# Two small setup products as 32-output matmuls, a label multiply placed earlier on GpSimd, and VectorE's first clears in pieces

## The chip, the cores and the metric

The kernel runs on one core of a Trainium2 chip. The metric is the device time of one execution in microseconds, median over several runs. A core has a matrix engine (TensorE, PE in the profile, with its weight loads shown apart as PEld), three engines for element-wise work (VectorE or DVE, ScalarE or ACT, GpSimd or POOL), and SyncE (SP), which here only issues DMAs. Each engine takes its instructions in order; between engines they wait on semaphores.

## The reference

A graph-attention layer over B = 16 batches of N = 512 nodes with F = 512 features, H = 16 heads of 32, two directions d, and only the first 20 nodes of each batch as keys and values. All in fp32.

```
row_zero  = v.sum(-1) == 0
q_exp     = where(row_zero, 0, q)                      # the condition, per node
self_feat = concat(v, q_exp) @ W_self.T + b_self
for d in 0, 1:
    A    = adj (or its transpose)[:, :, :20, :]        # 11 labels per pair
    cond = A.sum(-1);  vb = A @ w_bias + b_bias
    kv   = self_feat[:, :20]
    aff  = (self_feat @ Wq.T + bq) . (kv @ Wk.T + bk) / sqrt(32)   # per head
    aff  = where(cond > 0, aff, -9e15) + vb
    w    = softmax(aff over the 20 keys)
    out += per head: (w @ kv) @ Wout + bout
result = v + relu(self_feat + out)
```

The labels `adj` (the mask input) are integers; the sum over labels and the weighted sum with `w_bias` are needed for each batch.

## The kernel before, in words

The order of work on every engine is the order in which the code is written; no scheduler changes it. The first 90 us are the setup, after which a loop over the batches runs.

The setup has these steps:

- *Key rows* (L775 to L831). `xkv` holds the 320 key rows (16 x 20), transposed. GpSimd adds its four chunks into `rsk`. TensorE multiplies the rows with `W_self` (`kv_terms`, L781, weights 128 wide, 320 columns), the condition with its part of `W_self` (L791, four groups of 16 outputs into `ps_q`), then sums `rsk` over the partitions with a matrix of ones (L795, into `ps_nk`: every output row is the same sum). ScalarE copies `ps_q` into `q4` (L797). TensorE selects from `q4` with a 0/1 matrix `sel` (L800, one matmul for each of C = 4 chunks, 16 columns), which turns the condition round so that features lie on partitions. VectorE makes `nzk`, the flag of a nonzero key row (L798), copies the selection into `qw` (L801), and with products `qp` (L807) joins it to the key rows: `kvn` (L811), and `kvD`, differences to the first key (L815). TensorE goes on with the last five `kv_terms` and then with the key projections `key_rows` (L831, groups of four matmuls with 32 outputs each).
- *Bursts* n = 0 to 19 (the loop `for n, runs in enumerate(bursts)`). Each burst folds the projected keys into Wq (`keys`, L930, into a pair of PSUM tiles), ScalarE and VectorE copy the result to a stage `st` (L952, L954), and SyncE stores a finished stage to DRAM, `g_d` (L959, L961). There are sixteen stages (fc, hg); those with hg = 0, 1, 2 share three buffers in turn. Between the bursts stands other work, dealt out by the string `plan`: "v" and "w" make values (L893), "c" makes key biases (`bias_scores`: ScalarE's copy L871, GpSimd's sum L875, four small stores L877 to `cq_d`), "n" the row flags, "p" the self products of batch 0.
- *Batch 0's masks.* `mask_mul(0, 0)` turns the labels into floats on ScalarE (L323) and multiplies them by `w_bias` on GpSimd (L324); `mask_count` sums the labels on VectorE (L332) and GpSimd writes the -9e15 terms (L333); `mask_sum` reduces on VectorE (L338). `load_cq` (L128, SyncE) brings the key biases back from `cq_d`.
- *Blocks.* `clear_first` (L154) clears a DRAM area `bd_d` with one DMA issued by GpSimd; `spill` (L193, from n = 14 on, on GpSimd's and SyncE's queues) copies the values `vw_d` into it.

The first instructions on VectorE are three clears: `ones`, one half of `ps_q`, and `bqbd` (L723 to L726); `ones` starts seven warm-up matmuls on TensorE (L737).

Of the kernel before, what the change touches and what calls it, by code (L numbers as in the profile page):

```python
# [13 lines left out]
P = 128  # L14
# [4 lines left out]
def gat_kernel(  # L19
# [20 lines left out]
    nc = tc.nc  # L40
    B, F, N = xT.shape
    NG, L = adj.shape[3], adj.shape[4]
    H, DH = 16, 32
    C = F // P
    HL = P // DH
# [105 lines left out]
    def clear_first():  # L151

        n = C * EARLY * 32 // P
        nc.gpsimd.dma_start(  # L154
            bd_d[0].rearrange("c b r e i g -> (c b r) (e i g)").rearrange("(n p) w -> p n w", p=P),
            zero.unsqueeze(1).to_broadcast([P, n, HL * 2 * DH]),
        )
# [9 lines left out]
    def blocks(n):  # L167

        found = []
        bb = bd_d[n].rearrange("c b r e i g -> (c b) r e i g")  # L170
        vv = vw_d[n].rearrange("d c (b m) (e g) -> d (c b) m e g", m=NG, e=HL)
        for e in range(HL):
            for i in range(2):
                j = (e * S) // 32 + i
                for d in range(2):
                    lo = max(e * S + d * NG, 32 * j)
                    hi = min(e * S + (d + 1) * NG, 32 * j + 32)
                    if lo < hi:
                        m, r = lo - e * S - d * NG, lo - 32 * j
                        found.append((bb[:, r : r + hi - lo, e, i], vv[d, :, m : m + hi - lo, e]))  # L180
        return found
# [133 lines left out]
    def mask_mul(b, h, labels=range(11)):  # L315
        a = adjs[b, h].rearrange("p t (m l) -> p (t m) l", l=L)
        if labels[0] == 0:
            prods[b, h] = (msk if h == 0 or b == 0 else xsum).tile(
                [P, 2 * S, L + 1], F32, tag="prod", name=f"prod{b}_{h}", bufs=1
            )  # L320
        p = prods[b, h]
        if b == 0:
            nc.scalar.copy(p[:, :, :L], a)  # L323
            nc.gpsimd.tensor_mul(p[:, :, :L], p[:, :, :L], wb_sb.unsqueeze(1).to_broadcast([P, 2 * S, L]))  # L324
        else:
            for l in labels:
                nc.scalar.activation(p[:, :, l], a[:, :, l], AF.Identity, scale=wb_sb[:, l : l + 1])  # L327
# [371 lines left out]
    with tc.tile_pool(name="setup", bufs=1) as sp, tc.tile_pool(name="ps_acc", bufs=4, space=PSUM) as acc["pool"]:  # L699
# [18 lines left out]
        with tc.tile_pool(name="setup_k", bufs=1) as sk:  # L718
# [3 lines left out]

            nc.vector.memset(ones, 1.0)  # L723
            ps_q = ps_s.tile([P, 2, 512], F32, tag="s0", name="ps_q4", bufs=1)
            nc.vector.memset(ps_q[:, 0], 0.0)
            nc.vector.memset(bqbd, 0.0)  # L726
            nc.gpsimd.memset(zero, 0.0)

            nc.gpsimd.memset(sel, 0.0)
# [62 lines left out]
                    ps_q[bass.ds(k * DH, B), 0], q_sb[:, k], ws_q[:, k], start=True, stop=True  # L792
                )
            ps_n = ps_s.tile([P, 2, 512], F32, tag="s1", name="ps_nk", bufs=1)[:, 0]
            nc.tensor.matmul(ps_n[:, :BM], ones, rsk, start=True, stop=True)  # L795
            q4 = sk.tile([P, F], F32, name="q4")
            nc.scalar.copy(q4, ps_q[:, 0])  # L797
            nc.vector.tensor_scalar(nzk, ps_n[:, :BM], 0.0, None, ALU.not_equal)  # L798
            for c in range(C):
                nc.tensor.matmul(ps_q[:, 1, bass.ts(c, B)], q4[:, bass.ts(c, P)], sel, start=True, stop=True)  # L800
            nc.vector.tensor_copy(qw, ps_q[:, 1, : C * B].rearrange("p (c b) -> p c b", b=B))  # L801
            for fc, k in ((0, 3), (1, 3), (2, 3), (3, 2), (3, 3)):
                kv_terms(fc, k)
# [56 lines left out]
        with tc.tile_pool(name="setup_g", bufs=3) as sg:  # L860
# [60 lines left out]
            def keys(runs):  # L921


                pairs = [ps_s.tile([P, 2, 512], F32, tag=f"s{i}", name=f"ps_g{runs[0]}{i}", bufs=1) for i in range(2)]
                at = 0
                for fc, hg, d, lo, hi in runs:
                    n = (hi - lo) * ND
                    for hl in range(HL):
                        r = bass.ts(hl, DH)
                        nc.tensor.matmul(  # L930
                            pairs[hl // 2][:, hl % 2, at : at + n], wq_sb[r, d, hg, bass.ts(fc, P)],
                            khD[r, d * C + hg, lo * ND : hi * ND], start=at == 0, stop=True, skip_group_check=True,
                        )
                    at += n
                if not units and runs is bursts[-1]:
                    for hl in range(HL):
                        r = bass.ts(hl, DH)
                        nc.tensor.matmul(
                            pairs[hl // 2][:, hl % 2, at:], wq_sb[r, 0, 0, :P], khD[r, 0, : 512 - at],
                            start=False, stop=True, skip_group_check=True,  # L940
                        )
                at = 0
                for fc, hg, d, lo, hi in runs:
                    n = (hi - lo) * ND
                    if (fc, hg) not in stages:
                        stages[fc, hg] = (late if hg == C - 1 else sg).tile([P, B, HL, 2, ND], F32, tag="st", name=f"st{fc}{hg}")
                    st = stages[fc, hg]
                    for half in range(2):
                        to = st[:, lo:hi, bass.ts(half, 2), d].rearrange("p b h m -> p h b m")
                        of = pairs[half][:, :, at : at + n].rearrange("p h (b m) -> p h b m", m=ND)  # L950
                        if half == 0:
                            nc.scalar.activation(to, of, AF.Copy, scale=SCALE)  # L952
                        else:
                            nc.vector.tensor_scalar(to, of, SCALE, None, ALU.mult)  # L954
                    at += n
                    if d == 1 and hi == B:
                        to, of = g0[:, fc, bass.ts(hg, WD // C)], st[:, 0].rearrange("p h d m -> p (h d m)")
                        nc.gpsimd.tensor_copy(to, of)
                        nc.sync.dma_start(g1_d[C * fc + hg], st[:, 1].rearrange("p h d m -> p (h d m)"))  # L959
                        if fc * hg < (C - 1) * (C - 1):  # L960
                            nc.sync.dma_start(g_d[C * fc + hg], st[:, 2:])  # L961
# [44 lines left out]
            for n, runs in enumerate(bursts):  # L1006
                for i in range(len(rest)):
                    if (i < 1 and n > 0) or any(fc == 0 and (d, hg) == rest[0] for fc, hg, d, _, _ in runs):
                        key_rows(*rest.pop(0))
                if n in (3, 4):  # L1010
                    values(*steps["v"].pop(0)[1])
                if n == 0:
                    bo_rows = load.tile([P, C, N], F32, tag="x2", name="bo_rows", bufs=1)
                    nc.sync.dma_start(bo_rows[:, :2], bout.partition_broadcast(P))
                keys(runs)
                if n == 8:
                    mask_count(0, 0)
                if n == 14:
                    mask_count(0, 1)
                if n == 17:  # L1020
                    mask_sum(0, 1)
                value_pieces()
                if rest:
                    for kind in "mm" if n else ():
                        f, args = steps[kind].pop(0)
                        f(*args)
                    continue
                first = n if first is None else first
                for kind in plan[n - first] if n - first < len(plan) else ():
                    f, args = steps[kind].pop(0)  # L1030
                    f(*args)
                    if kind == "w":
                        value_pieces()
                if n == first:
                    for d in range(2):
                        nc.gpsimd.tensor_add(br_sb, br_sb, bo_rows[:, d])
                if n > first:
                    value_pieces()
                if n == 7:
                    mask_mul(0, 0)  # L1040
                if n == 10:
                    mask_sum(0, 0)
                    load_cq(0)
                if n == 7:
                    clear_first()
                if n == 9:
                    row_sums(1)
                    copies = blocks(0)
                if n > 13:
                    spill(1, nc.gpsimd)  # L1050
                    spill(1)
                if n == 11:
                    mask_mul(0, 1)
                    new_self(0)
                    for i in range(1, 5):
                        x_sum(0, i)
                if 10 < n < 15:
                    mask_spread(0, 0, (n - 11,))
                if n == 16:
                    gs[0] = g0  # L1060
                    key_sum(0, 1)
                    load_adj(1, 0)
                if n == 18:
                    mask_spread(0, 1)
                    key_bias(0)
                    load_adj(1, 1)
                    load_cq(1)
# [357 lines left out]
```

## Time and profile before

| | |
|---|---|
| time, median of 3 runs | 549.41 us (548.23 to 549.83) |
| the profiled execution | 548.23 us, its span 546.2 us |
| TensorE busy | 540.2 us, 99% of the span |
| VectorE, ScalarE, GpSimd busy | 481.3, 404.1, 434.3 us |
| granted TensorE clock | 0.996 of full |
| bytes moved by DMA | 126.45 MB, 232 GB/s over the span |

In the rows of a timeline stand the start in us, the busy time in us, the engine, the line, the operation and what it writes and reads, how many were merged, and in brackets how long the engine had been idle before and what ended that. Rows of groups give the busy time and the mean of one instruction in ns. SPq and POOLq are DMA queues by the engine that issues. In the rows of windows each engine has its busy time in the stretch and, in brackets, how many of its instructions touch it; the last three numbers are the granted clock, the share of the DMA engines' time, and GB/s.

### The profile page before, as it was taken

How to read it: one execution, taken by the hardware profiler on the slowest of the kernel's cores; microseconds unless marked ns; L12 is line 12 of the kernel's file. 1: busy time of each engine (PE TensorE's matmuls, PEld its weight loads, DVE VectorE, ACT ScalarE, POOL GpSimd, SP SyncE). 2: the span in 40 equal slices, each digit the busy share in tenths (PEclk: the TensorE clock that was granted, in tenths of full speed). 3: DMA queues.
4: the chain of work that ended last, by engine and by line, in shares of the span. 5: the costliest groups of instructions: out<-in, count | busy, mean ns of one | idle time of the engine just before them, and what ended most of it. 6: DMA issues, size and time to landing. Idle time of an engine off the chain costs nothing.

```text
span 546.2 us, 19673 instructions
## 1 busy us (share of the span) xinstructions
PE 540.2 (99%) x7932; PEld 423.7 (78%) x7932; DVE 481.3 (88%) x711; ACT 404.1 (74%) x999; POOL 434.3 (80%) x418
## 2 busy tenths in 40 slices
PE   9999999999999999999999999999999999999996
PEld 6544368889888878787888878887878788878784
DVE  1776678889999999999989999999999999999997
ACT  1225435888887979788888888888878787978664
POOL 2637996779979797979798888888897979797664
PEclk9999999999999999999999999999999999999998
DMA  8999999978886877878776758676777777736034
GB/s 306 377 396 355 314 360 342 311 259 251 226 255 190 250 194 225 227 217 233 220 219 192 236 180 232 203 231 188 231 210 210 194 230 191 240 92 200 2 116 156
DMA packets 100546, 126.45 MB, mean 232 GB/s; under 512 B 19608, under 2 KB 68694, under 8 KB 98408
## 3 DMA queue, kind: packets, MB, share of 16 engines
q1 hardware_dynamic: 98856, 122.19, 72.2%
q0 software_dynamic: 1168, 2.23, 1.8%
q8 instruction: 62, 1.02, 0.8%
q10 hardware_dynamic: 432, 0.79, 0.4%
q14 instruction: 28, 0.23, 0.1%
HBM read 86.23 MB, written 40.24 MB: 232 GB/s over the span
## 4 chain that ended last, share of the span: by engine, by line
PE 97%; DVE 2%; ACT 0%; issue 0%; DVEq 0%
PE ps_f L667 32%; PE ps_a L397 24%; PE ps_c L397 11%; PE ps_d L397 6%; PE ps_o_f L569 5%; PE ps_v L893 3%; PE ps_k L831 3%; PE ps_kv L781 2%; PE ps_a L284 1%; PE ps_o_c L569 1%; PE ps_l L397 1%; PE ps_c L284 1%; PE ps_warm L737 1%; PE ps_o_s L569 0%; DVE o L611 0%; DVE w L465 0%
## 5 line engine op out<-in xcount | busy, mean ns | idle before, releaser
L327 ACT ACTIVATE prod<-adj,wb_sb 128x80 f32<-128x80 int32 x330 | 116.0, 429 | 0.0
L537 POOL TENSOR_TENSOR w<-w,sm 128x640 f32<-128x640 f32 x63 | 80.3, 1275 | 33.0 <-DVE sm L533 29.3
L667 PE MATMUL ps_f<-t,ws_s 128*64 128x246 f32 x720 | 80.0, 370 | 0.0
L667 PEld LDWEIGHTS ps_f<-t,ws_s 128*64 128x64 f32 x720 | 51.7, 136 | 18.9
L528 ACT ACTIVATE w<-w 128x640 f32<-128x640 f32 x60 | 43.9, 731 | 18.0 <-DVE w L524 18.0
L545 DVE STREAM_TRANSPOSE wt<-w 128x640 f32<-128x640 f32 x63 | 52.5, 834 | 0.1
L667 PE MATMUL ps_f<-x,ws_v 128*64 128x246 f32 x480 | 52.4, 371 | 0.0
L532 DVE TENSOR_REDUCE sm<-w 128x32 f32<-128x640 f32 x63 | 51.1, 811 | 1.1 <-ACT w L528 0.8
L523 DVE TENSOR_REDUCE ps_d<-w 128x32 f32<-128x640 f32 x59 | 48.7, 826 | 1.8 <-ACT ps_d L431 0.2
L524 DVE TENSOR_TENSOR w<-w,ps_d 128x640 f32<-128x640 f32 x59 | 48.4, 821 | 2.0
L370 POOL TENSOR_TENSOR k<-g,k 128x608 f32<-128x608 f32 x30 | 44.8, 1492 | 0.0
L667 PEld LDWEIGHTS ps_f<-x,ws_v 128*64 128x64 f32 x480 | 34.7, 137 | 13.0
L397 PEld LDWEIGHTS ps_a<-g,sf 128*64 128x64 f32 x544 | 34.2, 137 | 5.9 <-issue 5.8
L397 PE MATMUL ps_a<-g,sf 128*64 128x152 f32 x544 | 38.6, 295 | 0.0
L397 PE MATMUL ps_d<-g,sf 128*64 128x152 f32 x544 | 37.9, 293 | 0.0
L346 ACT COPY both<-add 64x80 f32<-64x80 f32 x128 | 32.6, 254 | 5.7 <-DVE add L338 4.6
L569 PE MATMUL ps_o_c<-wt,vd 32*32 32x256 f32 (+1 forms) x720 | 36.8, 386 | 0.0
L338 DVE TENSOR_REDUCE add<-prod 128x80 f32<-128x960 f32 x32 | 36.7, 1146 | 0.0
L682 POOL TENSOR_TENSOR t<-x,t 128x492 f32<-128x492 f32 x30 | 34.9, 1163 | 1.2
L397 PEld LDWEIGHTS ps_d<-g,sf 128*64 128x64 f32 x544 | 35.3, 137 | 0.2 <-ACT sf L685 0.2
L333 POOL TENSOR_SCALAR prod<-cond 128x80 f32<-128x80 f32 x32 | 18.1, 566 | 21.7 <-DVE cond L332 20.2
L569 PE MATMUL ps_o_f<-wt,vd 32*32 32x256 f32 (+1 forms) x672 | 34.6, 386 | 0.0
(300 smaller groups left out, 1435.8 us busy)
## 6 DMA issues: line engine op xcount, KB each, us to landing
g<-g_d SPq DMA_DIRECT2D x60, 304.0 KB
g_d<-st SPq DMA_DIRECT2D x16, 1064.0 KB
out_T<-o SPq DMA_DIRECT2D x64, 256.0 KB
x<-in_xT SPq DMA_DIRECT2D x56, 256.0 KB
xn<-in_xn SPq DMA_DIRECT2D x48, 256.0 KB
adj<-in_adj SPq DMA_DIRECT2D x52, 220.0 KB
vd<-bd_d SPq DMA_DIRECT2D x64, 64.0 KB
nz<-nz_d SPq DMA_DIRECT2D x14, 256.0 KB
```

What stands on the lines that cost most here:

```text
L327: nc.scalar.activation(p[:, :, l], a[:, :, l], AF.Identity, scale=wb_sb[:, l : l + 1])
L338: done["masks"] = nc.vector.tensor_reduce(add, prods.pop((b, h)), AX.X, ALU.add)
L370: done["ksum"] = engine.tensor_sub(to, one, two)
L397: nc.tensor.matmul(slot(g)[bass.ts(p, P // 2), : HL * S].rearrange("p (h m) -> p h m", m=NG)[:, :, 1:], of(k)[:, bass.ds(first + g * P // ...
L523: nc.vector.tensor_reduce(mx, f, AX.X, ALU.max)
L524: done["weigh"] = (engine or nc.vector).tensor_sub(f, f, mx.unsqueeze(2).to_broadcast([P, per, NG]))
L528: done["exp"] = nc.scalar.activation(t, t, AF.Exp)
L532: nc.vector.tensor_reduce(sm, heads(weighs[b, c, l]), AX.X, ALU.add)
L537: done["normal"] = nc.gpsimd.tensor_mul(f, f, smalls.pop((b, c, l)).unsqueeze(2).to_broadcast([P, per, NG]))
L545: done["turn"] = nc.vector.transpose(wts[b][:, c, l], weighs.pop((b, c, l)).rearrange("p g w -> p (g w)"))
L569: nc.tensor.matmul(outsum[b][a][bass.ds(at // 2 * DH, n * DH), bass.ds(c * N // 2 + lo * R, (hi - lo) * R)].rearrange("p (n r) -> p n r", ...
L667: nc.tensor.matmul(parts[b][n in (2, 3, 5)][bass.ts(a, P // 2), bass.ts(i, HN)], lhs, x[:, k], start=False, stop=k == 1, skip_group_check= ...
```

## The change

Four edits in the setup:

- VectorE's clear of `ps_q` is made in four pieces of 128 columns, that of `bqbd` in four pieces.
- The sum of the key rows (L795) becomes four matmuls with 32 outputs each, and each of the four selecting matmuls (L800) becomes four with 32 outputs.
- `mask_mul(0, 0)` moves, within burst 7, from after the values' stores to right after `keys(runs)`.
- `clear_first()` moves from the end of burst 7 to burst 11.

```diff
             ps_q = ps_s.tile([P, 2, 512], F32, tag="s0", name="ps_q4", bufs=1)
-            nc.vector.memset(ps_q[:, 0], 0.0)
-            nc.vector.memset(bqbd, 0.0)
+            for a in range(HL):
+                nc.vector.memset(ps_q[:, 0, bass.ts(a, F // HL)], 0.0)
+            for c in range(C):
+                nc.vector.memset(bqbd[:, :, c], 0.0)
...
-            nc.tensor.matmul(ps_n[:, :BM], ones, rsk, start=True, stop=True)
+            for a in range(HL):
+                nc.tensor.matmul(ps_n[bass.ts(a, R), :BM], ones[:, :R], rsk, start=True, stop=True)
...
             for c in range(C):
-                nc.tensor.matmul(ps_q[:, 1, bass.ts(c, B)], q4[:, bass.ts(c, P)], sel, start=True, stop=True)
+                for a in range(HL):
+                    nc.tensor.matmul(
+                        ps_q[bass.ts(a, R), 1, bass.ts(c, B)], q4[:, bass.ds(c * P + a * R, R)], sel, start=True, stop=True
+                    )
...
                 keys(runs)
+                if n == 7:
+                    mask_mul(0, 0)
                 if n == 8:
                     mask_count(0, 0)
...
-                if n == 7:
-                    mask_mul(0, 0)
                 if n == 10:
                     mask_sum(0, 0)
                     load_cq(0)
-                if n == 7:
-                    clear_first()
                 if n == 9:
                     row_sums(1)
                     copies = blocks(0)
+                if n == 11:
+                    clear_first()
```

On TensorE, at the end of the key rows' products (ps_nk is the sum, the second ps_q row the selection; the sizes are outputs x columns). Before:

```order
L781 MATMUL ps_kv_185<-xkv,ws_v 128x320
L791 MATMUL ps_q_124<-ws_q,q_sb 16x512 x4
L795 MATMUL ps_nk<-rsk,ones 128x320
L800 MATMUL ps_q_124<-sel,q_204 128x16 x4
L781 MATMUL ps_kv_183<-xkv,ws_v 128x320
L781 MATMUL ps_kv_184<-xkv,ws_v 128x320
```

Now (the changed file's lines are 2 to 6 higher):

```order
L783 MATMUL ps_kv_191<-xkv,ws_v 128x320
L793 MATMUL ps_q_124<-ws_q,q_sb 16x512 x4
L798 MATMUL ps_nk<-rsk,ones 32x320 x4
L804 MATMUL ps_q_124<-sel,q_213 32x16 x16
L783 MATMUL ps_kv_189<-xkv,ws_v 128x320
L783 MATMUL ps_kv_190<-xkv,ws_v 128x320
```

The order is the same; the sum and the selection stand there as four and sixteen matmuls instead of one and four.

On GpSimd, in bursts 7 to 11 (the second key biases c and their stores to cq_d, the labels' product prod, the clear of bd_d, the row sums rx of batch 1). Before:

```order
L958 COPY g_84<-st_582 128x152
L875 TENSOR_TENSOR c<-c,bb_sb 128x320
L877 DMA cq_d<-c 4x16x20 x4
L324 TENSOR_TENSOR prod_0_648<-prod_0_648,wb_sb 128x80x11
L154 DMA bd_d_89<-zero 128x5x256
L958 COPY g_84<-st_625 128x152
L333 TENSOR_SCALAR prod_0_648<-cond_0_676 128x80
L913 DMA vw_d_88<-v_694 128x4x128
L215 TENSOR_TENSOR rx_728<-x_176 128x512
L217 TENSOR_TENSOR rx_728<-rx_728,x_176 128x512 x2
L913 DMA vw_d_88<-v_793 128x4x128
L324 TENSOR_TENSOR prod_1_796<-prod_1_796,wb_sb 128x80x11
```

Now:

```order
L964 COPY g_84<-st_603 128x152
L324 TENSOR_TENSOR prod_0_649<-prod_0_649,wb_sb 128x80x11
L881 TENSOR_TENSOR c<-c,bb_sb 128x320
L883 DMA cq_d<-c 4x16x20 x4
L964 COPY g_84<-st_646 128x152
L333 TENSOR_SCALAR prod_0_649<-cond_0_696 128x80
L919 DMA vw_d_88<-v_714 128x4x128
L215 TENSOR_TENSOR rx_748<-x_182 128x512
L217 TENSOR_TENSOR rx_748<-rx_748,x_182 128x512 x2
L919 DMA vw_d_88<-v_813 128x4x128
L154 DMA bd_d_89<-zero 128x5x256
L324 TENSOR_TENSOR prod_1_817<-prod_1_817,wb_sb 128x80x11
```

The product of the first labels moved ahead of the second key biases and their four stores, and the clear moved behind the row sums, to right before the second labels' product. On ScalarE the labels' cast (L323) likewise moved ahead of the copy of the second key biases (L871).

## The prediction

> **What bounds the kernel now.** I read the first part of the page, then the chain of waits, and only then the two stretches of the setup in which the edits lie.
>
> ```profile
> span 546.2 us, 19673 instructions
> PE 540.2 (99%) x7932; PEld 423.7 (78%) x7932; DVE 481.3 (88%) x711; ACT 404.1 (74%) x999; POOL 434.3 (80%) x418
> PE 97%; DVE 2%; ACT 0%; issue 0%; DVEq 0%
> ```
>
> TensorE is busy in 99% of the span and makes 97% of the chain that ended last. So an edit pays only by what it takes off TensorE's own sequence, or costs what it puts into it; time saved on VectorE, ScalarE or GpSimd is worth nothing unless TensorE waits for it. Next the chain and the timeline at 10 to 17 us, where the two matmul edits lie:
>
> ```profile
> 10.96 0.98 PE ps_q L791 x8
> 11.94 0.74 PE ps_nk L795 x2
> 12.68 1.03 PE ps_q L800 x8
> 13.71 2.79 PE ps_kv L781 x10
> ...
> 10.89 1.05 PE L791 MATMUL ps_q<-ws_q,q_sb 128*16 128x512 f32 x8
> 11.87 0.30 PEld L795 LDWEIGHTS ps_nk<-rsk,ones 128*128 128x128 f32 x2 [0.85 <-issue]
> 12.01 0.59 ACT L797 COPY q<-ps_q 128x512 f32<-128x512 f32 x1 [8.53 <-PE ps_q L791]
> 12.64 0.97 PEld L800 LDWEIGHTS ps_q<-sel,q 128*128 128x128 f32 x8 [0.48 <-ACT q L797]
> 12.72 0.49 DVE L798 TENSOR_SCALAR nzk<-ps_nk 128x320 f32<-128x320 f32 x1 [10.82 <-PE ps_nk L795]
> 13.53 2.46 PEld L781 LDWEIGHTS ps_kv<-xkv,ws_v 128*128 128x128 f32 x10
> 13.82 0.23 DVE L801 COPY qw<-ps_q 128x64 f32<-128x64 f32 x1 [0.62 <-PE ps_q L800]
> 15.21 0.97 DVE L815 TENSOR_TENSOR kvD<-kvn 128x304 f32<-128x304 f32 x1
> 16.43 1.18 PEld L831 LDWEIGHTS ps_k<-kvD,wk 128*32 128x32 f32 x24 [0.44 <-issue]
> ```
>
> Each fp32 matmul stands as two records. The selection (L800) can't begin before ScalarE's copy of q4 ends at 12.01 + 0.59 = 12.60; that is the one true wait here. After it come eight weight loads, and the key products' next load starts at 13.53.
>
> **The key rows' sum (L795).** One matmul with 128 outputs becomes four with 32 over the same 320 columns. Whatever it gains, 0.1 us or 0.3 us, TensorE then stands before the selection, which waits for q4 until 12.60, and q4 needs only L791. On TensorE's sequence it is worth 0. It would cost only from the point where the four end after 12.60, that is if they ran one after another: 3 more x 0.74 = 2.2 us. The groups of weight loads and two slices of 20 ns say that they do not:
>
> ```profile
> L831 PEld LDWEIGHTS ps_k<-kvD,wk 128*32 128x32 f32 x60 | 1.8, 110 | 2.1 <-issue 0.4
> L800 PEld LDWEIGHTS ps_q<-sel,q 128*128 128x128 f32 x8 | 1.0, 191 | 0.5 <-ACT q L797 0.5
> ...
> 16.46:16.48 0.02, 0.02 (x5) 0.02 (x8) 0.02 (x1) 0.00 (x0) 0.02 (x1) 1.00 0.28 102
> 16.50:16.52 0.02, 0.02 (x4) 0.02 (x8) 0.02 (x1) 0.00 (x0) 0.02 (x1) 1.00 1.42 512
> ```
>
> In the key products L831, which already have this 32-output form, eight loads and four matmuls are in flight 0.03 us after the first load began at 16.43: the four column groups run side by side.
>
> **The selection (L800).** Four matmuls of 16 columns become sixteen, each with a quarter of the weights: 32 records instead of 8. Before, eight loads take (13.53 - 12.64) / 8 = 0.111 us each; with only 16 columns to stream behind, the load is the cost. A 32-wide load lasts 110 ns against 191 ns, 81 ns less for 96 columns, so 0.84 ns a column: 27 ns of pure loading instead of 108, and about 4 ns beside it, 31 ns a record. From below: four groups side by side, 8 records each, 8 x 0.031 = 0.25 us. From above: no overlap at all, 32 x 0.031 = 1.0 us. In between lies the closest packing of small matmuls that the trace shows, in the chain:
>
> ```profile
> 35.70 0.10 PE _g(0, 2, 0, 14, 16)0_449 L930 x2
> 35.80 0.01 PE _g(0, 2, 0, 14, 16)1_450 L930 x2
> ```
>
> Four records of 38 columns in 0.11 us, 27 ns each, which would make 32 x 0.027 = 0.86 us. But those have 128-wide loads of 108 ns in four row groups, 108 / 4 = 27, so this is a load bound and not a pace of issue. I take 0.40 us, nearer to the lower end, since the loads at 16.43 start within 10 ns of each other.
>
> Behind it the array goes from 32-wide to 128-wide weights, which was not so before at this place. The price is in the rows above: the 128-wide load at 11.87 starts 0.07 us before the last 16-wide matmul ends (10.89 + 1.05 = 11.94), while the one at 13.53 starts 0.18 us before the selection's last ends (13.71). The switch costs 0.11 us. (The one before L795 goes away, but there q4 covers it.) So the next key products load at 12.64 + 0.40 + 0.11 = 13.15 instead of 13.53: **0.38 us off TensorE's sequence**; by the bounds 0.53 off or 0.22 on.
>
> Does the 0.38 last? What TensorE needs next is kvD at 16.43, now 16.05. VectorE's link starts with qw at 13.82, which follows the selection by 0.11 us and moves 0.38 to 0.49 earlier; nzk was done at 12.72 + 0.49 = 13.21 and is out of the way if the sum ends only 0.1 us sooner. kvD's first quarter, now ending at 15.21 + 0.97 = 16.18, comes at about 15.7. From there on the chain is TensorE's without a gap until the last 20 us, so the gain is carried to the end.
>
> **VectorE's clears.**
>
> ```profile
> 1.09 0.48 DVE L725 MEMSET ps_q<- 128x512 f32 x1
> 1.62 0.27 DVE L726 MEMSET bqbd<- 128x256 f32 x1
> ```
>
> Two become eight. If each piece cost as much as its whole, 4 x 0.75 = 3.0 us, VectorE would be done at 4.1 us; the first reader is L791 at 10.89 and VectorE's own next work is at 12.72. Cover of over 6 us: 0, gain or loss.
>
> **GpSimd's order at 55 to 76 us.** Here the multiply goes ahead of the second half of the key biases (sum L875 and four stores L877), and the clearing DMA goes behind the row sums.
>
> ```profile
> 55.04 0.72 POOL L875 TENSOR_TENSOR c<-c,bb_sb 128x320 f32<-128x320 f32 x1
> 56.06 2.55 POOL L877 DMA_DIRECT2D cq_d<-c  x4 [0.29 <-POOL c L875]
> 58.63 2.11 POOL L324 TENSOR_TENSOR prod<-prod,wb_sb 128x880 f32<-128x880 f32 x1
> 60.67 0.96 POOL L154 DMA_DIRECT2D bd_d<-zero  x1
> 68.81 2.11 POOL L324 TENSOR_TENSOR prod<-prod,wb_sb 128x880 f32<-128x880 f32 x1
> 72.00 1.14 POOL L257 TENSOR_TENSOR t<-x,t 128x492 f32<-128x492 f32 x1
> 85.94 0.31 POOL L958 COPY g<-st 128x152 f32<-128x152 f32 x1 [2.92 <-ACT st L952]
> ...
> 63.88 2.07 SPq L128 DMA_DIRECT2D cq<-cq_d  x2
> 66.07 1.65 SPq L959 DMA_DIRECT2D g_d<-st  x1
> 67.83 1.19 SPq L961 DMA_DIRECT2D g_d<-st  x1
> SPq L128 <- DMA cq_d<-c: 2.9, 1, 2.9
> bd_d<-zero POOLq DMA_DIRECT2D x1, 640.0 KB, 8.4
> 76.15 1.07 ACT L952 ACTIVATE st<-s_g(3, 0, 0, 0, 16)0_912 128x608 f32<-128x608 f32 x2 [1.79 <-POOL g L958]
> ```
>
> GpSimd has the same work in another order, so from 68.8 us on it stands where it stood: the x sums that TensorE's self products read come when they came. The second biases' stores are issued 2.11 us later. SyncE already waits 2.9 us for them at L128, in a queue that is in order; behind it stand the stage stores L959 and L961. So SyncE comes free at 68.1 instead of 66.0. The clear, 640 KB, lands 8.4 us after its issue, now about 67.9 + 8.4 = 76.3; the first block copies, issued at 76 to 78 us, wait for it, by some tenths. The masks themselves come earlier, but nobody waits for them before the seeds at 89 us. I put the whole edit at 0, covered by the late stores' slack: the stage buffer stored at 66 to 69 us is written again at 76.15 us.
>
> **The sum.** -0.38 (selection and switch) + 0 + 0 + 0. The profiled execution took 548.23 us (span 546.2), so 547.85; it was the fastest of three, and their median is 549.41, 1.18 above it. Against that median: 549.41 - 0.38 = **549.0 us**, 0.07% less. A measurement of this kernel tells no less than about 0.3% (1.6 us) from no change, so I forecast no visible difference.
>
> **Rivals.**
>
> *A. The selection is bound by issue.* If no two small matmuls start closer than the 27 ns seen at 35.70, it takes 0.86 + 0.11 instead of 0.89: +0.08, time 549.5 us. For it: nothing in the trace is packed closer over a long run. Against: the starts at 16.43. The Trainium skill, TensorE: Matmul & The Clock Gate (Wait — 56ns, not 53.3ns?), says that starts of matmuls never come closer than about 25 ns however few columns they stream, and TensorEngine Tiling (Instruction Overhead) warns against splitting a dimension that is already small; by the first figure an estimate is 0.80 us, no gain once the switch is paid. No run here shows such a long train of 16-column matmuls yet. Chance 0.25.
>
> *B. The late stores stall the stages; slower.* The delayed biases hold SyncE 2.1 us, and the clear puts 640 KB among the stores. Slices of 2 us:
>
> ```profile
> 68.00:70.00 2.00, 2.00 (x36) 1.04 (x28) 1.76 (x3) 0.52 (x2) 1.98 (x3) 1.00 0.65 205
> 70.00:72.00 2.00, 2.00 (x28) 1.14 (x20) 1.28 (x3) 1.37 (x4) 1.92 (x2) 1.00 1.02 402
> 72.00:74.00 2.00, 2.00 (x26) 1.29 (x28) 1.75 (x4) 0.96 (x2) 2.00 (x2) 1.00 1.07 422
> ```
>
> At 0.41 MB/us the clear is 1.6 us of all DMA engines, so the store of stage (2,0), 1064 KB, is up to 3.7 us late. It decides if that store landed after 76.15 - 0.38 - 3.7 + 0.7 = 72.8 us before (0.7 is what TensorE's 1.8 us of products between bursts leave over the 1.07 us copy). Issued at 67.8 to 69.0, its bytes are through by some 72 us. If it took the 8.4 us of the clear, it landed at 76.2, and the stall is 3.4 us: 549.0 + 3.4 = 552.4 us. Against it: the engines are only 0.65 busy at 68 to 70 us, room for part of the clear. Chance 0.08.
>
> *C. The change does nothing on TensorE's sequence:* something that I read as covered, kvD or a landing of weights, binds at 16 us instead, and the 0.38 turns into a wait: 549.4 us. Chance 0.12.
>
> The forecast itself has 0.55. All but B lie within 0.3%. What the runs scatter by (548.23 to 549.83) decides the edges: faster 0.05, within 0.3% 0.89, slower 0.06. Range 547.5 to 550.3: the forecast with its bounds (-0.15, +0.60) and the runs' scatter (-1.2, +0.4) is 547.7 to 550.0, a little widened for the smaller stalls of B.
>
> **What would show it.** Right: in the changed profile the selection's 32 records span about 0.4 us from 12.6, the next key products load near 13.15, and the chain's later pieces stand some 0.4 us earlier, at 90 us too. Issue-bound: the selection spans 0.8 us or more. B: ScalarE's and VectorE's stage copies at 76 to 85 us wait for a DMA of g_d, and TensorE has gaps there. Wrong altogether: the biases' load at L128 no later than 63.9 us, or a difference above 1.6 us with TensorE's setup unchanged.

## The result, and the profile after

The changed kernel takes 549.86 us (median of 22 runs, 548.42 to 551.23); the kernel before, in 22 runs beside them, 549.21 us (548.16 to 550.41). The ratio is **1.0015, with a 95% interval of 1.0008 to 1.0022**: slower by 0.8 us by the ratio (the medians differ by 0.65). That is within the 0.3% that I had called no visible difference, but on the other side of zero from the 0.38 us that I had forecast as a gain. Of the two profiled executions the one after took 549.0 us (span 547.1), 0.8 us more than the one before.

The page of the changed kernel, its span, the engines' busy time, and the shares of the chain of work that ended last:

```profile
span 547.1 us, 19739 instructions
PE 539.6 (99%) x7962; PEld 423.1 (77%) x7962; DVE 482.3 (88%) x717; ACT 404.6 (74%) x999; POOL 434.3 (79%) x418
PE 94%; DMA 2%; DVE 2%; ACT 0%; issue 0%; SPq 0%; DVEq 0%; ACTq 0%
```

TensorE's part of the chain fell from 97% to 94%, and there is a DMA in it now (2%), where before there was none. Its busy time is 0.6 us less while the span is 0.9 us longer, so TensorE waits somewhere where it did not before. First the place where the gain was forecast, in the timeline of TensorE's weight loads and VectorE (start, busy time, engine, line, operation, count, idle before):

```profile
1.01 0.96 DVE L726 MEMSET ps_q<- 128x128 f32 x4
1.98 0.33 DVE L728 MEMSET bqbd<- 128x64 f32 x4
10.34 0.29 PEld L793 LDWEIGHTS ps_q<-ws_q,q_sb 128*16 128x16 f32 x8 [0.44 <-issue]
12.23 0.35 PEld L804 LDWEIGHTS ps_q<-sel,q 128*32 128x32 f32 x32 [0.74 <-ACT q L800]
12.61 2.45 PEld L783 LDWEIGHTS ps_kv<-xkv,ws_v 128*128 128x128 f32 x10
```

The selection's 32 records take 0.38 us, from 12.23 to the key products' load at 12.61; before it was 0.89 (12.64 to 13.53). The key rows' sum needs no row: the load of the selection still waits for ScalarE's copy of q4. VectorE has its clears done at 2.31 us, 8 us before L793 needs them. So far everything is as forecast, and rather better. The gain also passes on to the key projections, where rival C would have lost it: their first load stands 16.43 - 12.64 = 3.79 us behind the selection's before, and 15.50 - 12.23 = 3.27 us now:

```profile
15.50 2.46 PEld L837 LDWEIGHTS ps_k<-kvD,wk 128*32 128x32 f32 x44 [0.44 <-issue]
```

Then the chain of waits of the same kernel, from 73.94 us on (start, length, what):

```profile
73.94 12.65 DMA g_d<-st
86.59 0.02 issue
86.61 0.04 ACTq L958
86.65 0.04 issue
86.70 0.41 ACT st L958
87.11 0.04 issue
87.15 0.41 PE _g(3, 3, 0, 7, 16)0_1082 L936 x2
```

The 2% DMA is one transfer: the store of stage (2,3) to g_d, issued at 73.94, landed at 86.59. The late stage buffer is free only then; ScalarE's copy of the next stage into it starts at 86.70, and TensorE's products behind it at 87.15. The timeline says how long each stood (ScalarE, VectorE, TensorE and SyncE's queue):

```profile
64.39 1.71 SPq L128 DMA_DIRECT2D cq<-cq_d  x2
73.94 1.69 SPq L967 DMA_DIRECT2D g_d<-st  x1
86.70 0.40 ACT L958 ACTIVATE st<-g(3, 2, 0, 14, 16)0_1033 128x266 f32<-128x266 f32 x1 [1.88 <-DMA g_d<-st]
86.72 0.44 DVE L960 TENSOR_SCALAR st<-g(3, 2, 0, 14, 16)1_1034 128x266 f32<-128x266 f32 x1 [1.48 <-DMA g_d<-st]
87.15 0.41 PE L936 MATMUL _g(3, 3, 0, 7, 16)0_1082<-khD,wq_sb 32*128 32x171 f32 x2 [1.07 <-ACT st L958]
```

In the profile shown of before, the same copies wait for nothing but TensorE's own products:

```profile
74.75 1.17 SPq L961 DMA_DIRECT2D g_d<-st  x1
84.81 1.11 ACT L952 ACTIVATE st<-g(3, 2, 0, 14, 16)0_1012 128x76 f32<-128x76 f32 x3 [1.91 <-PE g(3, 2, 0, 14, 16)1_1013 L930]
```

So TensorE stands 1.07 us behind ScalarE, ScalarE 1.88 us behind the store. The store was **not issued later** than before (73.94 against 74.75); it landed later: the semaphore events of the two traces have it complete at 84.80 before, 0.72 us ahead of the copy into its buffer at 85.52, and at 86.59 now. And the biases' load L128, which I had thought could hold SyncE, begins 0.5 us later than before (64.39 against 63.88; 0.9 later counted from the selection's first load), not 2.1. What differs is what the DMA engines did before that. Windows of the changed kernel (the last three numbers: granted clock, share of the DMA engines' time, GB/s):

```profile
64.00:68.00 4.00, 4.00 (x45) 1.25 (x36) 3.01 (x6) 3.05 (x8) 3.90 (x6) 1.00 0.60 201
68.00:72.00 4.00, 4.00 (x60) 2.61 (x56) 3.00 (x7) 1.37 (x4) 3.92 (x4) 1.00 1.01 379
84.00:88.00 4.00, 2.93 (x39) 2.33 (x40) 2.44 (x6) 2.06 (x7) 1.60 (x3) 1.00 1.04 335
```

The same windows before:

```profile
64.00:68.00 4.00, 4.00 (x56) 1.51 (x52) 2.67 (x6) 3.06 (x8) 3.84 (x4) 1.00 0.98 334
68.00:72.00 4.00, 4.00 (x56) 2.19 (x48) 3.04 (x6) 1.90 (x6) 3.90 (x4) 1.00 0.83 304
84.00:88.00 4.00, 4.00 (x62) 3.17 (x60) 2.93 (x8) 2.22 (x8) 1.60 (x3) 1.00 1.06 323
```

While SyncE stands at the biases' load, the stage stores stand behind it. Before, the clear of bd_d (640 KB, issued at 60.67) went through in that gap, and the engines were 0.98 busy. Now the clear, whose move the title does not name, is issued at 66.80, the gap is 0.60 full, and (0.98 - 0.60) x 4 us = 1.5 us of DMA work is left for later. The next 4 us take up (1.01 - 0.83) x 4 = 0.7 us of it; behind them the engines are full in both kernels, and the store of (2,3) lands 1.8 us later than in this profile of before and 1.0 later than in a second one (85.60, before_2 below). The buffers ahead of it are closer too: the copy into (3,2) waits 0.46 us for the store of (2,2), but TensorE isn't held there.

### The profile page after: what moved, and what is told of

The parts are those of the page before. It is cut to its first block, busy times and chain, and to the rows that moved or that the text cites. A ratio compares the mean times of both kernels' runs of the same rounds, so it can differ in the third digit from the quotient of the medians.

```text
span 547.1 us, 19739 instructions
## 1 busy us (share of the span) xinstructions
PE 539.6 (99%) x7962; PEld 423.1 (77%) x7962; DVE 482.3 (88%) x717; ACT 404.6 (74%) x999; POOL 434.3 (79%) x418
## 4 chain that ended last, share of the span: by engine, by line
PE 94%; DMA 2%; DVE 2%; ACT 0%; issue 0%; SPq 0%; DVEq 0%; ACTq 0%
PE ps_f L667 32%; PE ps_a L397 24%; PE ps_c L397 11%; PE ps_d L397 6%; PE ps_o_f L569 5%; PE ps_v L899 3%; PE ps_k L837 3%; DMA g_d<-st 2%; PE ps_kv L783 2%; PE ps_o_c L569 1%; PE ps_l L397 1%; PE ps_warm L739 1%; PE ps_o_s L569 0%; DVE o L611 0%; DVE w L465 0%; PE ps_c L284 0%
```

## The experiments

Theory **C** (called S in the first expectations): the clear at burst 11 competes with the stage stores instead of filling the gap ahead of them, the store of (2,3) lands later, and the wait eats the 0.5 us that the matmuls won. Rival **M**: the labels' multiply, now ahead of the second biases, makes SyncE late at L128 and the stores with it. Rival **L**: the 32-output matmuls, or a loop that runs slower behind them, cost the time by themselves. Rival **A** from the prediction: small matmuls are bound by issue. Two more came up on the way: **G**, that GpSimd's own stores wait for each other, and **Q**, that SyncE standing at L128 makes the gap and with it the late landing. The matmuls, the clear and the multiply were each run alone, and the clear was also taken back alone; VectorE's smaller clears were not run by themselves. In all of it "setup" is the time from the first load of q4's products (L791 or, changed, L793) to the loop's first seed (L427 on ScalarE); it leaves out what comes before, which scatters from execution to execution.

**e1_mm: the two matmul edits alone**

```diff
-            nc.tensor.matmul(ps_n[:, :BM], ones, rsk, start=True, stop=True)
+            for a in range(HL):
+                nc.tensor.matmul(ps_n[bass.ts(a, R), :BM], ones[:, :R], rsk, start=True, stop=True)
...
-                nc.tensor.matmul(ps_q[:, 1, bass.ts(c, B)], q4[:, bass.ts(c, P)], sel, start=True, stop=True)
+                for a in range(HL):
+                    nc.tensor.matmul(
+                        ps_q[bass.ts(a, R), 1, bass.ts(c, B)], q4[:, bass.ds(c * P + a * R, R)], sel, start=True, stop=True
+                    )
```

> Only the two matmul edits. Theory S (the clear in burst 11 adds 640 KB to the stage stores, stage (2,3)'s store lands late, and the copies into stage (3,3), which shares its buffer, hold TensorE at 86 us): no clear moved, so TensorE keeps its 0.4 us unless that store was already close: ratio 0.9992 to 1.0000 (-0.4 to 0 us). Rival M (the multiply ahead of the key biases holds SyncE's queue): the same. Rival L (the 32-output matmuls themselves, or a loop that runs slower after them, cost the 0.8 us): ratio 1.0010 or more.

Measured: 550.0 us against 549.16, ratio 1.0015 (1.0006 to 1.0024). The part that should have been the gain is, alone, a loss, in the range of L and outside that of S and M. The timeline of GpSimd and of TensorE's loads in e1_mm:

```profile
49.84 2.52 POOL L881 DMA_DIRECT2D cq_d<-c  x4 [0.29 <-POOL c L879]
52.34 1.49 POOL L917 DMA_DIRECT2D vw_d<-v  x2
55.12 1.29 POOL L881 DMA_DIRECT2D cq_d<-c  x2 [0.29 <-POOL c L879]
58.37 1.24 POOL L881 DMA_DIRECT2D cq_d<-c  x2 [1.96 <-DMA cq_d<-c]
68.85 0.16 PEld L222 LDWEIGHTS ps_nz<-rx,ones 128*32 128x32 f32 x8 [1.48 <-POOL rx L217]
```

GpSimd's ninth store of this stretch (4 + 2 + 2 are ahead of it) waited 1.96 us until the first had landed, 8.3 us after its issue. The trace's instructions say why the first: GpSimd's DMAs signal eight semaphores in turn (111 to 118), and the ninth store itself waits for 113, which the store eight ahead of it signals and which it will signal next. GpSimd's row sums came late by that; TensorE's load waited 1.48 us for them, against 0.63 in the profile of before, and its matmuls stood still for 1.0 us between 64 and 72 us, where before they had no gap. The page of e1_mm has 2% of the chain on these stores and 2% on GpSimd. The prediction did not look here; it is a second place where the setup hangs on a landing.

**e13_mm_vw: the same two matmul edits, and the values' stores of one piece on SyncE's queue**

```diff
-                            nc.gpsimd.dma_start(
+                            (nc.sync if (t, d) == (0, 1) else nc.gpsimd).dma_start(
```

> The two matmul edits, and the value stores of the first key tile's direction 1 on SyncE's queue instead of GpSimd's. In the run of the matmul edits alone GpSimd's third store of the second key biases stood 1.96 us until the first store of the first biases had landed, the row sums came late and TensorE waited 1.48 us for them. Theory G (GpSimd's stores in flight): with two stores fewer in that queue and 1.5 us less work on GpSimd the wait goes, and with it the loss: ratio 0.9990 to 1.0003 and no wait of TensorE for the row sums. Rival L (the 32-output matmuls make what follows slower): ratio 1.0010 to 1.0020 stays.

Measured: 548.97 us against 549.12, ratio 1.0004 (0.9990 to 1.0018). In its timeline the second biases' four stores follow each other without a wait, and TensorE doesn't wait for rx:

```profile
50.63 2.51 POOL L881 DMA_DIRECT2D cq_d<-c  x4 [0.29 <-POOL c L879]
54.43 2.48 POOL L881 DMA_DIRECT2D cq_d<-c  x4 [0.29 <-POOL c L879]
67.40 0.13 PEld L222 LDWEIGHTS ps_nz<-rx,ones 128*32 128x32 f32 x4 [0.30 <-issue]
```

With two of the eight stores ahead of the ninth gone from GpSimd, the wait is gone. The setup is 77.58 us, against 78.10 and 78.08 in the two profiles of before: 0.5 us shorter, which is the selection's whole gain. Its time lies between what G and L had forecast, and the two ratios' intervals overlap, so it is the rows that show the wait and its removal, not the times.

**e2_clear: the clear at burst 11 alone**

```diff
-                if n == 7:
-                    clear_first()
...
+                if n == 11:
+                    clear_first()
```

> Only the clear in burst 11. S: +0.8 to +1.5 us, ratio 1.0015 to 1.0027, and a copy into stage (3,3) that waits for a DMA of g_d at 85 to 87 us. M and L: 0, ratio within 0.9995 to 1.0005.

Measured: 549.22 us against 549.16, ratio 1.0002 (0.9993 to 1.0011): no loss, so in time the expectation of S was missed. Its profiled execution nevertheless has the wait. The window in which SyncE stands, and ScalarE's copy into the late buffer:

```profile
64.00:68.00 4.00, 4.00 (x52) 1.53 (x52) 2.75 (x6) 3.15 (x8) 3.84 (x5) 1.00 0.73 237
```

```profile
87.23 0.40 ACT L952 ACTIVATE st<-g(3, 2, 0, 14, 16)0_1012 128x266 f32<-128x266 f32 x1 [1.68 <-DMA g_d<-st]
```

Its setup is 79.67 us, of which 0.4 us are a later start of the selection, most of it a wait for q4's weights, which come long before the clear (12.56 - 10.38 = 2.18 us from the first load to the selection, 1.75 before). One execution shows the mechanism, eleven do not show its price.

**e3_mul: the labels' multiply alone**

```diff
                 keys(runs)
+                if n == 7:
+                    mask_mul(0, 0)
...
-                if n == 7:
-                    mask_mul(0, 0)
```

> Only the label multiply moved ahead of the second key biases. S: 0 to +0.3 us (the biases' load on SyncE starts up to 2.1 us later, and the stores behind it catch up). M: +0.6 us or more, ratio 1.0011 or more. L: 0.

Measured: 548.73 us against 549.16, ratio 0.9993 (0.9984 to 1.0001); no copy into a stage buffer waits for a DMA. In its SyncE timeline L128 begins at 64.80, 0.92 us later than before, of which 0.72 is that this execution's L791 began later (11.61 against 10.89). M falls: the multiply costs nothing that these runs show.

**e4_clear_back and e4b_clear_back: the changed kernel with the clear at burst 7 again** (the same kernel on two chips)

```diff
+                if n == 7:
+                    clear_first()
...
-                if n == 11:
-                    clear_first()
```

> The changed kernel with the clear back at the end of burst 7, all else as changed. S: the loss goes away, -0.5 to +0.1 us against the kernel before, ratio 0.9991 to 1.0002. M and L: the loss stays, ratio 1.0010 to 1.0020.

> The changed kernel with the clear back in burst 7, a second time. C: at least 0.0010 below the changed kernel run beside it, ratio 0.9990 to 1.0005 to the kernel before. If the clear's place is not the cause: the same ratio as the changed kernel.

Measured: 548.63 us against 549.16, ratio 0.9998 (0.9987 to 1.0008; its profile fell on its longest execution, 551.21 us, so the rows below are the other's), and on the other chip 549.0 against 549.40, 0.9998 (0.9988 to 1.0008). Beside the second ran the changed kernel once more:

> The changed kernel again, beside the next one on the same chip. Theory C (the clear behind 66 us makes stage (2,3)'s store land about 1 us later, and the copies into stage (3,3) wait for it): ratio 1.0008 to 1.0020, a copy into stage (3,3) that waits 1 to 2 us for a DMA of g_d near 86.5 us. If the first result was an accident of the runs: ratio 0.9995 to 1.0005.

after_2: 549.89 us against 549.40, ratio 1.0020 (1.0007 to 1.0034). On one chip, then, moving the clear back is worth 549.89 - 549.0 = 0.9 us. L falls with it: the matmul edits are in e4_clear_back and e4b_clear_back too, and the loss isn't. The windows, of after_2:

```profile
64.00:68.00 4.00, 4.00 (x52) 1.61 (x48) 2.52 (x6) 2.91 (x8) 3.84 (x6) 1.00 0.63 233
```

and of e4b_clear_back:

```profile
64.00:68.00 4.00, 4.00 (x52) 1.60 (x48) 2.54 (x6) 2.93 (x8) 3.84 (x5) 1.00 0.99 349
```

The gap is filled where the clear is at burst 7 and not where it is at burst 11. But the wait is not gone in e4b_clear_back, only shorter:

```profile
86.73 0.40 ACT L958 ACTIVATE st<-g(3, 2, 0, 14, 16)0_1033 128x266 f32<-128x266 f32 x1 [0.98 <-DMA g_d<-st]
```

It waits 0.98 us here and 1.39 in after_2, and even a second profile of the kernel before, **before_2**, waits 0.52 at 85.70:

> The kernel before once more, for its profile: its first profile fell on its second fastest execution of 22. If a typical execution has DMA waits in the setup too, this one shows a copy into a stage, a GpSimd store or the flags of batch 2 waiting for a DMA, and a span above 546.2 us; if the balance of the first profile is typical, none over 0.6 us.

That execution took 548.28 us, with a setup of 78.08; TensorE did not stand for it. So the late buffer's store is on the edge already in the kernel before, 0.72 us clear of the copy in one profile and 0.52 us behind it in the other: whatever makes the work ahead shorter, or the transfer later, runs into it.

**e8_after_cq: the biases' load behind burst 13; e14_back_cq: the same with the clear back.** If the gap at SyncE is the point (Q), moving the load that makes the gap should do as well as moving the clear back.

```diff
                 if n == 10:
                     mask_sum(0, 0)
+                if n == 13:
                     load_cq(0)
```

> The changed kernel with the key biases' load moved on SyncE from burst 10 to burst 13. Theory Q (SyncE standing at that load holds the stage stores, DMA engines idle at 64 to 68 us, and the bytes pile up later): the stores of stage (2,0) start 1 to 2 us earlier, the copy into stage (3,3) waits less, ratio 0.9993 to 1.0005. Theory C (the moved clear's 640 KB alone): about 0.3 us of the 0.8 at most comes back, ratio 1.0008 to 1.0016.

> The changed kernel with the clear back in burst 7 and the key biases' load in burst 13. If TensorE's sequence sets the setup once both DMA waits are gone: -0.4 to -0.6 us, ratio 0.9989 to 0.9997. If the DMA engines' bytes set it anyway: ratio 0.9996 to 1.0005.

Measured: e8_after_cq 549.93 us against 549.12, 1.0016 (1.0004 to 1.0029), in the range of C and not of Q; e14_back_cq 549.45, 1.0007 (0.9994 to 1.0020), where I had expected a gain of 0.4 to 0.6 us. SyncE's timeline of e8_after_cq:

```profile
72.89 2.88 SPq L128 DMA_DIRECT2D cq<-cq_d  x2
77.97 1.42 SPq L967 DMA_DIRECT2D g_d<-st  x1
```

The load now stands right ahead of the store that matters, which goes out 4 us later than in the changed kernel (73.94) and still lands at the same time, 86.7. So the landing did not follow the issue here. The two kernels differ in the clear's place alone. First e8_after_cq, then e14_back_cq:

```profile
64.00:68.00 4.00, 4.00 (x48) 1.53 (x48) 2.85 (x6) 3.24 (x8) 3.92 (x5) 1.00 0.99 372
86.77 0.40 ACT L958 ACTIVATE st<-g(3, 2, 0, 14, 16)0_1033 128x266 f32<-128x266 f32 x1 [1.32 <-DMA g_d<-st]
...
64.00:68.00 4.00, 4.00 (x52) 1.60 (x48) 2.52 (x6) 2.91 (x8) 3.84 (x5) 1.00 1.00 359
86.09 0.40 ACT L958 ACTIVATE st<-g(3, 2, 0, 14, 16)0_1033 128x266 f32<-128x266 f32 x1 [0.31 <-DMA g_d<-st]
```

The gap at 64 to 68 us is closed in both, and the wait is still there with the clear at burst 11. So that one gap is not the whole cause. In e8_after_cq the DMA engines are less busy later, 0.89 at 76 to 80 us against 1.00. Summed over 60 to 84 us, they are busy for 22.3 to 23.1 us in the four profiles with one clear at burst 11, and for 23.4 to 24.0 in the nine with it at burst 7. Theory C fits in this form: with the clear at burst 11 the engines get less done by then, wherever the gap falls. That this shortfall sets the landing is argued; that the landing is late with the clear there is shown in the table below.

**e11_clear2: the clear made twice at burst 11** (the second writes the same zeros over the first).

```diff
                 if n == 11:
                     clear_first()
+                    clear_first()
```

> The changed kernel with the clear made twice, back to back, in burst 11: 640 KB more in front of the stage stores. C: +1.0 to +1.6 us more (640 KB at 0.4 MB/us), ratio 1.0033 to 1.0045. If the queue has room for it: ratio 1.0010 to 1.0020 as without.

Measured: 554.6 us against 549.12, ratio 1.012 (1.009 to 1.015), beyond both expectations. It is no clean dose. GpSimd's timeline (of its longest execution, 559.08 us):

```profile
67.76 0.86 POOL L154 DMA_DIRECT2D bd_d<-zero  x1
79.10 0.88 POOL L154 DMA_DIRECT2D bd_d<-zero  x1 [10.48 <-DMA bd_d<-zero]
```

The second clear has the first one's destination and waited 10.48 us for it, with everything that GpSimd had behind it. The first of the two took 11.1 us to land, but the single clear took 7.6 in the changed kernel itself, and 6.7 to 11.1 in the profiles with it at burst 7 (8.4 before): how long the clear itself takes does not tell the two places apart.

**e17_back_vw: the changed kernel with the clear at burst 7 and the values' stores of one piece on SyncE**, which should take both waits away.

```diff
-                            nc.gpsimd.dma_start(
+                            (nc.sync if (t, d) == (0, 1) else nc.gpsimd).dma_start(
...
+                if n == 7:
+                    clear_first()
...
-                if n == 11:
-                    clear_first()
```

> The same with the value stores of the first key tile's direction 1 on SyncE's queue as well, so that GpSimd has 1.5 us less to do. If TensorE's wait for the row sums near 68 us (0.4 to 0.6 us) and the stage buffers are what is left: 0.2 to 0.6 us below the kernel before, ratio 0.9988 to 0.9997. If the bytes of the setup set the time: ratio 0.9996 to 1.0005.

Measured: 548.58 us (547.3 to 549.65) against 549.40, **ratio 0.9987 (0.9977 to 0.9997)**: faster than the kernel before and, on the same chip, than the changed one (549.89). Its window and ScalarE's copy into the late buffer:

```profile
64.00:68.00 4.00, 4.00 (x56) 1.71 (x52) 2.50 (x6) 2.80 (x8) 3.60 (x5) 1.00 1.03 389
```

```profile
85.06 1.11 ACT L958 ACTIVATE st<-g(3, 2, 0, 14, 16)0_1033 128x76 f32<-128x76 f32 x3 [1.91 <-PE g(3, 2, 0, 14, 16)1_1034 L936]
```

No copy waits for a store. The setup is 77.50 us. The setups of the profiled executions side by side: what ScalarE's copy or TensorE's load waited for, for how long TensorE's matmuls stood still between 60 and 88 us, and when the store of (2,3) had landed, counted from the selection's first load:

| kernel | clear in burst | first load of q4's products | first seed | setup, us | waits | TensorE still | (2,3) landed |
|---|---|---|---|---|---|---|---|
| before | 7 | 10.89 | 88.99 | 78.10 | none | 0 | 72.2 |
| before_2 | 7 | 10.45 | 88.53 | 78.08 | copy 0.52 | 0 | 73.4 |
| e3_mul | 7 | 11.61 | 89.69 | 78.08 | none | 0 | 72.1 |
| e1_mm | 7 | 10.22 | 89.90 | 79.68 | rx 1.48 | 1.00 | 70.0 |
| e13_mm_vw | 7 | 11.27 | 88.85 | 77.58 | copy 0.26 | 0 | 72.6 |
| e4_clear_back | 7 | 11.53 | 89.49 | 77.96 | copy 1.01 | 0.38 | 73.3 |
| e4b_clear_back | 7 | 11.61 | 89.55 | 77.94 | copy 0.98 | 0.35 | 73.3 |
| e14_back_cq | 7 | 11.64 | 89.13 | 77.49 | copy 0.31 | 0 | 72.6 |
| e17_back_vw | 7 | 11.74 | 89.24 | 77.50 | none | 0 | 71.9 |
| after | 11 | 10.34 | 89.52 | 79.18 | copy 1.88 | 1.07 | 74.4 |
| after_2 | 11 | 11.64 | 90.12 | 78.48 | copy 1.39 | 0.60 | 73.8 |
| e2_clear | 11 | 10.38 | 90.05 | 79.67 | copy 1.68 | 0.87 | 74.6 |
| e8_after_cq | 11 | 11.31 | 89.58 | 78.27 | copy 1.32 | 0.68 | 73.6 |

TensorE's loads for the row flags wait up to 0.63 us for rx in several of these, before among them, without a gap in its matmuls; these are not listed. In after, e1_mm and e2_clear the setup also holds 0.1 to 0.4 us of a later start of the selection, part of it a wait for q4's weights.

With the clear at burst 11 the store landed 73.6 to 74.6 us behind the selection's start in all four, with it at burst 7 at 73.4 at the latest in all nine. With the matmul edits and TensorE never still the setup is 77.5 to 77.6, 0.5 to 0.6 us under that of before. Where TensorE stands still for 0.6 us or more, that is gone.

## Why the prediction was wrong

**Right: the selection, and a little more.** The step "the next key products load at 12.64 + 0.40 + 0.11 = 13.15 instead of 13.53" gave a gain of 0.38 us. From the first load of q4's products to the key products' next load it was 13.53 - 10.89 = 2.64 us before, and 2.13 in after_2. Rows of after_2:

```profile
11.64 0.13 PEld L793 LDWEIGHTS ps_q<-ws_q,q_sb 128*16 128x16 f32 x8 [0.44 <-issue]
...
13.40 0.35 PEld L804 LDWEIGHTS ps_q<-sel,q 128*32 128x32 f32 x32 [0.76 <-ACT q L800]
13.77 1.37 PEld L783 LDWEIGHTS ps_kv<-xkv,ws_v 128*128 128x128 f32 x6
```

2.64 - 2.13 = 0.51. (In the first profile after it is 2.27: there the selection itself began later behind the first load, 1.89 us against 1.76.) The lower bound, 0.25 us plus the switch of 0.11, was right: 13.77 - 13.40 = 0.37, with the switch from 32-wide to 128-wide weights in it. The 0.40 + 0.11 that I took lay 0.14 above it: the term was mis-sized, on the safe side.

**Right: the key rows' sum at 0**, since q4 still ends last, and **VectorE's clears at 0** by the cover of 8 us; the latter were not run by themselves.

**Rival C is out**: the gain is still there at the key projections, 3.27 us behind the selection's start against 3.79. **Rival A is out.** 32 records in 0.37 us are 12 ns each, less than half the 27 ns by which it would have been bound. The Trainium skill, TensorE: Matmul & The Clock Gate (Wait — 56ns, not 53.3ns?), has starts no closer than about 25 ns; this train does not keep to that figure taken over all column groups, while within one group, eight records in 0.37 us, it is 46 ns. The Trainium skill, TensorEngine Tiling (Array Packing) (Key Properties), says that different tiles can load weights and multiply in parallel. The trace agrees as far as it goes: 32 loads in four groups took 0.37 us; how long one group alone takes no run shows.

**Wrong: "From there on the chain is TensorE's without a gap until the last 20 us, so the gain is carried to the end."** The chain does not say that. It names what ended last at each step, not by how much the next one missed it. At 84 to 88 us the store of (2,3) was only just met: it landed 0.72 us ahead of the copy in one profile of before, and in before_2, the same kernel, the copy waits 0.52 us for it. In e1_mm the gain of 0.5 us was given back at another such place, GpSimd's ninth store. The 0.51 us is real on TensorE's sequence; it reaches the loop's start in e13_mm_vw, e14_back_cq and e17_back_vw, where neither place holds TensorE. In the time only e17_back_vw shows it.

**Wrong: "I put the whole edit at 0, covered by the late stores' slack."** I had checked the slack of the buffer stored at 66 to 69 us, (2,0) to (3,0), and that held, though its store landed at 74.14 before and not "by some 72 us" (72.25 after, with the copy at 75.33). The one without slack is three stages on, (2,3) to (3,3). Rival B had the mechanism, a stage store late because of the clear, but for the wrong buffer, at a price of 3.4 us, and with more than half of the store's 3.7 us delay from SyncE: L128 came 0.5 us later than before, not 2.1. The clear's place is what counts beside the other edits, 0.9 us between after_2 and e4b_clear_back. I had worked out that the clear is 1.6 us of all DMA engines' time, and not asked where it used to be done: in a gap that the stage stores left.

The parts of the edit on GpSimd pull against each other. The matmul edits alone lose 0.8 us; with the multiply ahead of the biases they don't (0.9998 twice), and the changed kernel's four bias stores show no wait:

```profile
57.11 2.52 POOL L883 DMA_DIRECT2D cq_d<-c  x4 [0.29 <-POOL c L881]
```

They are issued 57.11 - 49.77 = 7.3 us after the first biases' stores, against 5.3 in e1_mm, and those land in 5.9 to 7.0 us. (Before, the two were 5.3 us apart as well and there was no wait, but only just: the store of semaphore 114 landed at 57.70, and the one that waits for it went out at 57.99.) So, by one profile each and the times, the multiply that I put at 0 saves what e1_mm lost, and the clear takes it back; why the first store landed later in e1_mm (8.3 us after its issue, 4.7 before) stays open. The clears in smaller pieces, which the changed kernel has and e1_mm has not, were not told apart from it.

**Open.** e2_clear lost nothing in time, while the same move costs 0.9 us beside the other edits; by the landing alone it should cost about the same in both. A possible reason, only argued, is that the matmul edits bring the copies 0.5 us sooner to a landing that stays; but e2_clear's own profile already waits 1.68 us. Where each execution's wait ends is also uneven (from none to 1.01 us with the clear at burst 7), so that a single profile can't settle a few tenths. The gain in time is thin too: e13_mm_vw and e14_back_cq have a setup as short as that of e17_back_vw, and their times are not below those of before (1.0004 and 1.0007, the intervals reach down to 0.9990 and 0.9994), so the 0.13% of e17_back_vw is one interval among many and may be partly luck. A further stage buffer, which should take the wait away without touching the DMA, wasn't tried.

## What to carry to other kernels

Weights that a small matmul loads in full but multiplies with few columns are worth splitting over TensorE's column groups: here 0.89 us became 0.37. Before a gain is carried to the end of a chain, look for waits that were only just met, in a second profile and at every buffer that is reused, and price the gain up to the nearest of them. A bulk transfer that nobody waits for can still stand in a place where it is free, a gap of the DMA engines; moved out of there, it can take time from transfers that somebody waits for.

## What the hardware showed that I had not expected

- GpSimd's ninth DMA waits until the one eight ahead has landed: 1.96 us in e1_mm, and in e2_clear the tenth waited 0.74 us for the second. It looks like a limit of the queue, but the wait is in the program, whose instructions go through eight semaphores in turn. Stores of 5 KB landed 4.5 to 8.3 us after issue in these two.
- A store's landing did not follow its issue: issued at 73.94 in after or at 77.97 in e8_after_cq, the (2,3) store landed at 86.6 to 86.7.
- The start of q4's products lies anywhere from 10.2 to 11.7 us with no relation to the edits (10.45 and 10.89 in two executions of the kernel before), and from VectorE's last output to the end it is 3.3 to 4.9 us. Together that is more than any effect here, so the setup had to be read from one instruction to another, and the times from eleven or more runs.
